# Half of the GRU's row transposes of layers one and two moved from TensorE to DMA, and the state update cut from three VectorE passes after z to two

## The chip, the cores and the metric

The kernel runs on one core of one Trainium2 chip. The metric is the device time of one execution in microseconds (us), as the median of several runs. Beside those runs one execution was profiled; every row of a profile and every duration below is from that one execution. A core has TensorE (PE in the profile, with its weight loads as PEld), VectorE (DVE), ScalarE (ACT), GpSimd (POOL) and SyncE (SP), which here only issues DMAs. They run their own instruction streams in order and wait for each other on semaphores.

## The reference, cut to what matters

There are 64 graphs of 256 nodes with 256 features. Four graph layers follow each other; each normalises `x`, applies relu, computes its layer and adds it to `x`. Layers 0, 1 and 2 are attention layers (4 heads, 4 heads, 1 head). Layer 3, in which the change lies, has three rounds of message passing with a GRU cell:

```python
def _gru_cell(inp, h, w_ih, w_hh, b_ih, b_hh):
    gi = inp @ w_ih.T + b_ih
    gh = h @ w_hh.T + b_hh
    i_r, i_z, i_n = jnp.split(gi, 3, axis=-1)
    h_r, h_z, h_n = jnp.split(gh, 3, axis=-1)
    r = jax.nn.sigmoid(i_r + h_r)
    z = jax.nn.sigmoid(i_z + h_z)
    n = jnp.tanh(i_n + r * h_n)
    return (1.0 - z) * n + z * h
...
A = (adj != 0).astype(x.dtype)
h = x
for i in range(3):
    m = jnp.einsum('bnd,de->bne', h, weight[i])
    aggr = jnp.einsum('bst,bsd->btd', A, m)
    h = _gru_cell(aggr, h, w_ih, w_hh, b_ih, b_hh)
return h
...
h = jnp.maximum(_layernorm(x, axis=-1), 0.0)
x = x + _L3_gnn_ref(h, adj, ...)
```

## The kernel before, in words

The work is cut into 33 units: units 1 to 31 hold two graphs each (512 nodes, S = 512), units 0 and 32 hold one. `graphs(u, first, nb)` (line 1021) records all operations of a unit: `layer0`, `layer1`, `layer2`, then `gru`. Nothing is emitted while it records. Each operation has an engine, a written-down cost in ns and the buffers that it reads and writes; buffers come from classes with a fixed number of slots (lines 853 to 864: 8 PSUM banks, 8 slots `g` for the gate tiles, 2 slots `hl`, 1 slot `y`, 2 slots `tp`, 3 slots `pl`).

The order of the instructions on each engine is made by a planner, `_Schedule.run` (line 681). It gives each operation a due time, worked back from its unit's end (unit number times `PACE`), with `STRETCH` and `MARGIN` as allowances per step. Then it walks through a planned time: whenever an engine is free, it takes from the ready operations the one with the earliest due time whose buffers have a free slot (`roomy`, line 654). `HOP` is the assumed delay from the end of an operation to the start of one that waits for it. `GUARDED` names a buffer class in which a later unit must leave a slot free while an earlier unit still has to take one; `YIELD` belongs to VectorE operations that give way to others. The resulting order is fixed in the program; on the chip each engine runs its list in order. Several units are in progress at once (there are five slots for `xt`), so that TensorE always has matmuls of one unit while ScalarE and VectorE work on others.

**The GRU** (line 1442). The state is held transposed, features on partitions, in two halves of 128 features (j = 0 and 1), as `ht3_`. For each of three rounds (i = 0, 1, 2; the code's L, called layers of the GRU here) and each half, `unit` (line 1548) issues six `gate` operations (line 1483), each two 128x512 matmuls in fp32 (the profile shows two records for each): r and z each from the state (`whh`) and from the aggregate (`wc`), the candidate's two parts apart. ScalarE evaluates the tanh of each (line 874, `vec`), VectorE combines them. Sigmoid is written through tanh: with t = tanh(half of the argument), z = (1 + t)/2. The new state is stored as twice its value, 2h' = (1 + t) h + (1 - t) n.

For the next round the aggregate needs the state with nodes on partitions again. `rows_of` (line 1514) turns a half: on TensorE it issues four 128x128 transposes into a PSUM bank (line 1523). `split` (line 1448) then makes a high and a low part from it (`hl`: one ScalarE copy, line 1452, one VectorE subtraction), and `aggregate` (line 1458) multiplies both parts by the adjacency matrix in eight matmuls (line 1465).

The other way to turn a half exists already, `rows_turned` (line 1493). ScalarE copies the 128x512 fp32 words into two planes of 16 bits (`pl`, line 1502), SP issues a DMA transpose of both planes (`tp`, line 1503), ScalarE copies the planes back into words (`y`, line 1507). It is used in units 1 to 31 (`BACK`), for the last round's result, where `y` is added to `x` directly. The tuple `EARLY` names the halves for which it is used in the first two rounds as well; before the change it is empty. The layers before the GRU turn their normalised rows in the same way (lines 1113, 1115, 1119).

**The normalisation** (`norm`, line 1035) of layers 0, 1 and 2 subtracts the mean of each 128-row chunk and applies relu: chunks named in `CENTRED` on VectorE (line 1053), the others on ScalarE (line 1057). The normalisation in front of the GRU scales on ScalarE always (line 1063).

```python
                    vec(stt, dve(683), lambda: by_chunk(d.tile), lambda: by_chunk(z.tile), 1.0,
                        lambda: block(ht, j), op0=OP.add, op1=OP.mult,
...
                    vec(stt, dve(683), lambda: n.tile, lambda: z.tile, -1.0, lambda: n.tile,
                        op0=OP.add, op1=OP.mult, reads=[z], writes=[n], port=True)
                    vec(stt, dve(683), lambda: h_new.tile[:, j, :], lambda: d.tile, 2 * half, lambda: n.tile,
                        op0=OP.mult, op1=OP.subtract, reads=[d, n], writes=[(h_new, j)], port=True)
```

These are the three VectorE passes after z (`d` = (t + 1) h, `n` = (t - 1) n, then the difference); the first and the second wait for z's tanh, the third for both.

Of the kernel before, what the change touches and what calls it, by code (L numbers as in the profile page):

```python
# [14 lines left out]
OP = mybir.AluOpType  # L15
# [505 lines left out]
TURNED = 3  # L521
ENDED = 1
CLOSED = 0
CENTRED = (0,1)
BACK = range(1, 32)
EARLY = ()
LIFTED = (0,2)
PACE = 101000.0


def _runs(numbers):
# [15 lines left out]
class _Op:  # L547
    __slots__ = (
        "engine", "cost", "port", "emit", "group", "bufs", "takes", "nbytes", "succs", "waits", "due", "ready",
        "index", "yields", "base", "grabs",  # L550
    )


class _Schedule:
# [9 lines left out]


    OVERLAP = {"pe": 0, "act": 97, "dve": 81, "pool": 0, "sp": 0}
    HOP = {"pe": 250, "act": 100, "dve": 200, "pool": 100, "sp": 0}
    DMA_LATENCY = 3500
    DMA_RATE = 220.0
    DMA_AHEAD = 2000  # L570
    RESERVE = {"dve": 1.0, "act": 1.03}
    STRETCH = 2.0
    MARGIN = 1600
    YIELD = 20000.0
    GUARDED = ("wh",)

    def __init__(self, tc, pools):

# [8 lines left out]
        return _Buf(cls, shape, dtype, tile)  # L587

    def op(self, engine, cost, emit, reads=(), writes=(), takes=(), nbytes=0, port=False, yields=False,
           grabs=False):  # L590
        o = _Op()
        o.port, o.yields, o.grabs = port or grabs, yields, grabs
        o.engine, o.base, o.emit, o.group, o.nbytes = engine, cost, emit, self.group, nbytes
        o.cost = cost * self.RESERVE.get(engine, 1.0)
        o.succs, o.index, o.ready = [], len(self.ops), 0.0
        deps, o.bufs, o.takes = set(), [], []
        for written, items in ((False, reads), (True, writes)):
            for item in items:
                b, part = item if isinstance(item, tuple) else (item, None)
                if b not in o.bufs:  # L600
                    o.bufs.append(b)
                    b.left += 1
                if written and b.tile is None and b not in o.takes:
                    o.takes.append(b)
                keys = list(b.parts) if part is None else [k for k in (part, None) if k in b.parts]
                for k in keys:
                    writer, readers = b.parts[k]
                    if writer is not None:
                        deps.add(writer)
                    if written:  # L610
                        deps.update(readers)
                writer, readers = b.parts.get(part, (None, []))
                if written:
                    if part is None:
                        b.parts.clear()
                    b.parts[part] = (o.index, [])
                else:
                    b.parts[part] = (writer, readers + [o.index])
        for b in takes:
            if b.tile is None and b not in o.takes:  # L620
                o.takes.append(b)
        deps.discard(o.index)
        o.waits = len(deps)
        for d in deps:
            self.ops[d].succs.append(o)
        self.ops.append(o)
        return o
# [26 lines left out]
    def roomy(self, o):  # L654
        need = {}
        for b in o.takes:
            if b.tile is None:
                need[b.cls] = need.get(b.cls, 0) + 1
        for c, n in need.items():
            if c in self.GUARDED and self.first_taker(c) < o.group:  # L660
                n += 1
            if len(self.free[c]) < n:
                return False
        return True
# [113 lines left out]
def _fast_path(  # L778
# [48 lines left out]
    slots = ctx.enter_context(tc.tile_pool(name="slots", bufs=1))  # L827
# [29 lines left out]
            "cap_n": (slots, 1), "xn": (slots, 4), "ht": (slots, 2), "wh": (slots, 3),  # L857
            "cb2_": (slots, 2), "cb1_": (slots, 1), "pt": (slots, 5), "o": (slots, 2),
            "ag": (slots, 2), "ht3_": (slots, 3), 
            "hl": (slots, 2), "am_r": (slots, 1), "g": (slots, 8), "y": (slots, 1), "f": (slots, 6),  # L860
            "st": (slots, 4), "mv": (slots, 5), "row": (slots, 3), "rs": (slots, 10),
            "mean": (slots, 4), "pl": (slots, 3), "tp": (slots, 2), "rd": (dram, 4), "bank": (banks, 8),
        },
    )
# [5 lines left out]
    def bank(dtype=F32):  # L870
        return buf("bank", [P, S * 4 // mybir.dt.size(dtype)], dtype)

    def vec(fn, cost, *args, reads=(), writes=(), engine="dve", port=False, yields=False, grabs=False, **kw):
        emit = lambda: fn(*[a() if callable(a) else a for a in args], **kw)  # L874
        op(engine, cost, emit, reads, writes, port=port, yields=yields, grabs=grabs)


    sched.group = -1
# [142 lines left out]
    def graphs(u, first, nb):  # L1021
# [420 lines left out]
        def gru(pair):  # L1442
# [33 lines left out]
            def by_chunk(ap):  # L1476
                return ap.rearrange("p (c n) -> p c n", n=P)
# [5 lines left out]
            def gate(ps, w, B_w, g, v, first, last):  # L1483
                def emit():
                    for dc in range(DC):
                        nc.tensor.matmul(  # L1486
                            by_chunk(ps.tile[:, :S]), lhsT=w[:, dc, g * P : (g + 1) * P], rhs=block(v, dc),
                            start=(first and dc == 0), stop=(last and dc == DC - 1),
                        )

                op("pe", pe(1717), emit, [v, B_w], [ps])

            def rows_turned(ht, j, last):

# [39 lines left out]
            def g_tile():  # L1534
                return buf("g", [P, S])
# [6 lines left out]
            for i in range(L):  # L1542
                last = i == L - 1
                h_new = buf("ht3_", [P, DC, S])
                wi = wc[:, i]
                stt = nc.vector.scalar_tensor_tensor

                def unit(j, ht, ag, h_new, wi, half):
                    r, n, d, z = (g_tile() for _ in range(4))
                    ps_r, ps_h, ps_i, ps_z = (bank() for _ in range(4))  # L1550
                    gate(ps_r, whh, B_whh, j, ht, True, False)
                    gate(ps_h, whh, B_whh, 4 + j, ht, True, True)
                    vec(nc.scalar.activation, act(682), lambda: n.tile, lambda: ps_h.tile[:, :S], AF.Identity,
                        bias=bg[:, 4 + j : 5 + j], scale=half, reads=[ps_h, B_bg], writes=[n], engine="act")
                    gate(ps_r, wi, B_wc, j, ag, False, True)
                    vec(nc.scalar.activation, act(682), lambda: r.tile, lambda: ps_r.tile[:, :S], AF.Tanh,
                        bias=bg[:, j : j + 1], scale=half, reads=[ps_r, B_bg], writes=[r], engine="act")
                    vec(stt, dve(683), lambda: n.tile, lambda: r.tile, 1.0, lambda: n.tile,
                        op0=OP.add, op1=OP.mult, reads=[r], writes=[n], port=True)
                    gate(ps_i, wi, B_wc, 4 + j, ag, True, True)  # L1560
                    vec(stt, dve(685), lambda: n.tile, lambda: ps_i.tile[:, :S], 2 * half, lambda: n.tile,
                        op0=OP.mult, op1=OP.add, reads=[ps_i], writes=[n])
                    vec(nc.scalar.activation, act(712), lambda: n.tile, lambda: n.tile, AF.Tanh,
                        bias=bg[:, 6 + j : 7 + j], reads=[B_bg], writes=[n], engine="act")
                    gate(ps_z, whh, B_whh, 2 + j, ht, True, False)
                    gate(ps_z, wi, B_wc, 2 + j, ag, False, True)
                    vec(nc.scalar.activation, act(682), lambda: z.tile, lambda: ps_z.tile[:, :S], AF.Tanh,
                        bias=bg[:, 2 + j : 3 + j], scale=half, reads=[ps_z, B_bg], writes=[z], engine="act")
                    vec(stt, dve(683), lambda: by_chunk(d.tile), lambda: by_chunk(z.tile), 1.0,
                        lambda: block(ht, j), op0=OP.add, op1=OP.mult,  # L1570
                        reads=[z, ht if len(ht.shape) == 4 else (ht, j)], writes=[d], port=True)
                    vec(stt, dve(683), lambda: n.tile, lambda: z.tile, -1.0, lambda: n.tile,
                        op0=OP.add, op1=OP.mult, reads=[z], writes=[n], port=True)
                    vec(stt, dve(683), lambda: h_new.tile[:, j, :], lambda: d.tile, 2 * half, lambda: n.tile,
                        op0=OP.mult, op1=OP.subtract, reads=[d, n], writes=[(h_new, j)], port=True)

                for j in range(DC):
                    unit(j, ht, ag, h_new, wi, 0.5 if i == 0 else 0.25)
                ag = None if last else buf("ag", [P, DC, S])
                for j in range(DC):  # L1580
                    hl = rows_of(h_new, j, last)
                    if not last:
                        aggregate(ag, [hl], j, lambda k, b, sc, hl=hl: hl.tile[:, k, 2 * b + sc, :])
                ht = h_new
# [85 lines left out]
```

## Time and profile before

| | us |
|---|---|
| median of 3 runs | 3029.45 (3028.26 to 3031.09) |
| the profiled execution, whole | 3031.28 |
| its span, first to last instruction | 3029.5 |
| granted TensorE clock, mean over the span | 0.997 |

| steady stretch, 500 to 2500 us | busy us of 2000 |
|---|---|
| PE | 2000.00 |
| DVE | 1554.03 |
| ACT | 1560.36 |
| POOL | 182.78 |

How to read the rows of the profile: a group is a line of the kernel, an engine, an operation and its tiles (`out<-in`, buffer numbers left out), then how often it occurs, its busy time, the mean duration of one in ns, and the engine's idle time just before it with what ended it. Most ScalarE and VectorE operations are issued through the helper `vec` and so stand under line 874; they are told apart by their tiles. PE records overlap, since a matmul's record lasts longer than the distance to the next one.

### The profile page before, as it was taken

What the parts mean: (1) busy time and instruction counts of PE and PEld (TensorE: products, weight loads), DVE (VectorE), ACT (ScalarE), POOL (GpSimd) and SP (SyncE); (2) the same over time, 40 slices, a digit from 0 to 9 for tenths busy, and PEclk for the clock granted to TensorE, in tenths of its full rate; (3) what the DMA queues carried; (4) which work ended last, traced back from release to release, by engine and by line L of the source; (5) the groups of instructions that cost most, each with busy time, mean ns of one, the idle gap of its engine ahead of it and who ended that gap; (6) DMA issues with size and microseconds to landing.
All of it is one profiled execution on the core that took longest, in us unless ns stands there. A gap on an engine that the chain in (4) does not pass through costs nothing.

```text
span 3029.5 us, 47896 instructions
## 1 busy us (share of the span) xinstructions
PE 2996.4 (99%) x17423; PEld 1813.7 (60%) x17423; DVE 2307.4 (76%) x5702; ACT 2260.7 (75%) x4123; POOL 283.2 (9%) x317
## 2 busy tenths in 40 slices
PE   7999999999999999999999999999999999999998
PEld 6865556656565656565656566555556565656556
DVE  8977887777877777887778877778877778877653
ACT  6867777787878788787787877877787877766544
POOL 2101010001100011000010100010010010100000
PEclk9999999999999999999999999999999999999999
DMA  4222222323323322232232223233233222221110
GB/s 140 76 64 65 60 74 74 90 69 78 72 64 84 85 67 74 70 81 77 68 94 60 74 74 91 69 82 72 59 84 84 68 72 68 65 67 46 39 30 19
DMA packets 429321, 215.86 MB, mean 71 GB/s; under 512 B 356170, under 2 KB 408980, under 8 KB 429076
## 3 DMA queue, kind: packets, MB, share of 16 engines
q1 hardware_dynamic: 425104, 211.36, 28.1%
q8 instruction: 139, 2.28, 0.3%
q10 hardware_dynamic: 3972, 1.36, 0.2%
q14 instruction: 106, 0.87, 0.1%
HBM read 109.84 MB, written 17.34 MB: 42 GB/s over the span
## 4 chain that ended last, share of the span: by engine, by line
PE 98%; DVE 1%; ACT 1%; DMA 0%; issue 0%; SPq 0%; ACTq 0%; DVEq 0%
PE bank L1486 65%; PE bank L1269 12%; PE bank L1137 11%; PE bank L1465 6%; PE bank L1523 2%; PE bank L994 1%; PE bank L1192 0%; PE bank L1172 0%; PE bank L1098 0%; DMA at<-in_adj_dram 0%; DVE o L874 0%; DVE pt L874 0%; DVE pt L1234 0%; ACT pt L1243 0%; DVE g L874 0%
## 5 line engine op out<-in xcount | busy, mean ns | idle before, releaser
L1486 PE MATMUL bank<-ht,whh 128*128 128x512 f32 (+1 forms) x2376 | 1052.8, 580 | 0.0
L1486 PE MATMUL bank<-ag,wc 128*128 128x512 f32 (+1 forms) x2376 | 1050.4, 580 | 0.0
L1486 PEld LDWEIGHTS bank<-ag,wc 128*128 128x128 f32 x2376 | 448.7, 190 | 524.4 <-issue 509.1
L1486 PEld LDWEIGHTS bank<-ht,whh 128*128 128x128 f32 x2376 | 441.5, 191 | 481.5 <-issue 451.7
L874 ACT ACTIVATE g<-bank,bg 128x512 f32<-128x512 f32 (+1 forms) x594 | 392.6, 671 | 207.3 <-PE bank L1486 202.7
L874 DVE SCALAR_TENSOR_TENSOR g<-g,g 128x512 f32<-128x512 f32 (+1 forms) x396 | 265.7, 671 | 264.5 <-ACT g L874 262.8
L1269 PE MATMUL bank<-wh,pt 128*64 128x65 f32 (+1 forms) x8704 | 372.3, 232 | 0.1
L1269 PEld LDWEIGHTS bank<-wh,pt 128*64 128x64 f32 (+1 forms) x8704 | 340.8, 141 | 50.3 <-POOL mean L874 20.5
L1243 ACT ACTIVATE pt<-cb,f 128x256 f32<-128x256 f32 x620 | 322.8, 590 | 0.6 <-DMA cb<-rd 0.6
L1119 ACT COPY ht<-tp 128x1024 uint16<-128x1024 uint16 x232 | 306.8, 1339 | 0.9 <-DMA tp<-pl 0.5
L874 DVE SCALAR_TENSOR_TENSOR pt<-pt,f,cap 128x256 f32<-128x256 f32 x620 | 264.7, 481 | 2.8 <-ACT pt L1243 2.6
L1147 ACT ACTIVATE wh<-bank,mv 128x264 f32<-128x264 f32 (+1 forms) x384 | 177.2, 479 | 85.8 <-PE bank L1137 85.1
L1465 PE MATMUL bank<-am_r,hl 128*128 128x256 f32 x1536 | 234.7, 302 | 0.9 <-ACT hl L1452 0.6
L1113 ACT COPY pl<-xn 128x1024 uint16<-128x1024 uint16 x232 | 234.9, 1036 | 0.8
L874 POOL TENSOR_TENSOR mv<-mv,nhalf 128x4 f32<-128x4 f32 (+1 forms) x132 | 136.9, 1044 | 1022.9 <-DVE mv L874 765.1
L1042 DVE BATCH_NORM_STATS2 st<-xt 128x6 f32<-128x256 f32 x512 | 207.1, 404 | 20.6 <-DMA xt<-in_x_dram 20.4
L1465 PEld LDWEIGHTS bank<-am_r,hl 128*128 128x128 f32 x1536 | 197.9, 189 | 28.0 <-issue 22.0
L874 DVE SCALAR_TENSOR_TENSOR g<-bank,g 128x512 f32<-128x512 f32 (+1 forms) x198 | 133.4, 674 | 102.0 <-PE bank L1486 100.8
L874 ACT ACTIVATE g<-g,bg 128x512 f32<-128x512 f32 (+1 forms) x198 | 139.5, 705 | 95.7 <-DVE g L874 94.8
L1234 DVE TENSOR_SCALAR pt<-cb,f 128x256 f32<-128x256 f32 x532 | 184.2, 408 | 31.9 <-DMA cb<-rd 30.0
L874 DVE SCALAR_TENSOR_TENSOR g<-g,ht 128x512 f32<-128x512 f32 (+1 forms) x198 | 133.2, 673 | 91.4 <-ACT g L874 91.2
L874 ACT COPY ag<-bank 128x512 f32<-128x512 f32 (+1 forms) x198 | 110.1, 572 | 84.0 <-PE bank L1465 83.0
(96 smaller groups left out, 3222.4 us busy)
## 6 DMA issues: line engine op xcount, KB each, us to landing
cb<-rd SPq DMA_DIRECT2D x120, 512.0 KB
xt<-in_x_dram SPq DMA_DIRECT2D x31, 512.0 KB
at<-in_adj_dram SPq DMA_DIRECT2D x31, 512.0 KB
out_dram<-xt SPq DMA_DIRECT2D x31, 512.0 KB
cb<-rd SPq DMA_DIRECT2D x34, 256.0 KB
tp<-pl SPq DMA_TRANSPOSE x294
cap<-cap_n SPq DMA_TRANSPOSE x128
rd<-row ACTq DMA_DIRECT2D x60, 8.0 KB
```

The lines of the kernel that those rows point to most:

```text
L874: emit = lambda: fn(*[a() if callable(a) else a for a in args], **kw)
L1042: nc.vector.bn_stats(st.tile[:, c, :], xt.tile[:, c, :])
L1113: op("act", 1040, lambda: nc.scalar.copy(pl.tile, planes(xns[b].tile.rearrange("p c d -> p (c d)"))), [xns[b]], [pl])
L1119: op("act", 1330, lambda: nc.scalar.copy(planes(ht.tile[:, 2 * b : 2 * b + 2].rearrange("p c d n -> p (c d n)")), tp.tile,), [tp], [(ht, b)])
L1137: nc.tensor.matmul(ps.tile[:, : heads * W], lhsT=ht.tile[:, c, dc, :], rhs=we[:, dc].rearrange("p h w -> p (h w)"), start=(dc == 0), stop= ...
L1147: op("act", 470, lambda: nc.scalar.activation(wh.tile[:, :, c, :], ps.tile[:, : heads * W].rearrange("p (h w) -> p h w", h=heads), AF.Iden ...
L1234: nc.vector.tensor_scalar(pt.tile[:, b, jc, :].rearrange("p (i n) -> p i n", n=P), cb.tile[:, k, 2 * b : 2 * b + 2, :], f.tile[:, 1, h, c ...
L1243: op("act", 590, lambda: nc.scalar.activation(view().rearrange("p (i n) -> p i n", n=P), cb.tile[:, k, 2 * b : 2 * b + 2, :], AF.Relu, sca ...
L1269: nc.tensor.matmul(ps[q * Q : (q + 1) * Q], lhsT=pt.tile[:, b, jc, i0 : i0 + Q], rhs=wh.tile[:, h, 2 * b + jc, :w], start=(jc == 0), stop= ...
L1465: nc.tensor.matmul(ps.tile[:, b * N : (b + 1) * N], lhsT=rows(k, b, sc), rhs=am.tile[:, 2 * b + sc, :], start=(k == 0 and sc == 0), stop=( ...
L1486: nc.tensor.matmul(by_chunk(ps.tile[:, :S]), lhsT=w[:, dc, g * P : (g + 1) * P], rhs=block(v, dc), start=(first and dc == 0), stop=(last a ...
L1523: nc.tensor.transpose(ps.tile[:, c * P : (c + 1) * P], ht.tile[:, j, c * P : (c + 1) * P], ident)
```

## The change

What it does:

- `EARLY = (0,)`: in units 1 to 31, half j = 0 is turned by `rows_turned` in the first two rounds too. Half j = 1 stays on TensorE.
- `unit` writes the state as 2h' = (t + 1)(h - n) + 2n. The difference `d` is made before z's tanh and lies in r's tile; after z two passes are left. The number of VectorE passes in a unit stays five. `unit` takes three `g` tiles in place of four; `leave` makes n's first operation wait in the plan until three `g` slots are free, and r's until two are.
- `CENTRED = ()`: the chunks 0 and 1 of the three attention layers' normalisations go from VectorE to ScalarE.
- The planner: `PACE` 101000 to 98000, `HOP` of PE 250 to 300, `STRETCH` 2 to 1, `YIELD` 20000 to 5000; `wh` is guarded no more; in the new class `STRICT`, which holds `hl`, no operation of a later unit takes a slot while an earlier unit still has to take one. `y` gets a second slot, `mv` a sixth. `LEAVE` is 0.

```diff
-CENTRED = (0,1)
+CENTRED = ()
 BACK = range(1, 32)
-EARLY = ()
+EARLY = (0,)
 LIFTED = (0,2)
-PACE = 101000.0
+LEAVE = 0
+PACE = 98000.0
...
-    HOP = {"pe": 250, "act": 100, "dve": 200, "pool": 100, "sp": 0}
+    HOP = {"pe": 300, "act": 100, "dve": 200, "pool": 100, "sp": 0}
...
-    STRETCH = 2.0
+    STRETCH = 1.0
     MARGIN = 1600
-    YIELD = 20000.0
-    GUARDED = ("wh",)
+    YIELD = 5000.0
+    GUARDED = ()
+    STRICT = ("hl",)
...
         for c, n in need.items():
-            if c in self.GUARDED and self.first_taker(c) < o.group:
+            n += o.leave
+            if (c in self.GUARDED or c in self.STRICT) and self.first_taker(c) < o.group:
+                if c in self.STRICT:
+                    return False
                 n += 1
             if len(self.free[c]) < n:
                 return False
...
-            "hl": (slots, 2), "am_r": (slots, 1), "g": (slots, 8), "y": (slots, 1), "f": (slots, 6),
-            "st": (slots, 4), "mv": (slots, 5), "row": (slots, 3), "rs": (slots, 10),
+            "hl": (slots, 2), "am_r": (slots, 1), "g": (slots, 8), "y": (slots, 2), "f": (slots, 6),
+            "st": (slots, 4), "mv": (slots, 6), "row": (slots, 3), "rs": (slots, 10),
...
-                    r, n, d, z = (g_tile() for _ in range(4))
+                    r, n, z = (g_tile() for _ in range(3))
+                    d = r
...
+                    vec(stt, dve(683), lambda: by_chunk(d.tile), lambda: block(ht, j), 2 * half,
+                        lambda: by_chunk(n.tile), op0=OP.mult, op1=OP.subtract,
+                        reads=[n, ht if len(ht.shape) == 4 else (ht, j)], writes=[d], port=True)
                     gate(ps_z, whh, B_whh, 2 + j, ht, True, False)
                     gate(ps_z, wi, B_wc, 2 + j, ag, False, True)
                     vec(nc.scalar.activation, act(682), lambda: z.tile, lambda: ps_z.tile[:, :S], AF.Tanh,
                         bias=bg[:, 2 + j : 3 + j], scale=half, reads=[ps_z, B_bg], writes=[z], engine="act")
-                    vec(stt, dve(683), lambda: by_chunk(d.tile), lambda: by_chunk(z.tile), 1.0,
-                        lambda: block(ht, j), op0=OP.add, op1=OP.mult,
-                        reads=[z, ht if len(ht.shape) == 4 else (ht, j)], writes=[d], port=True)
-                    vec(stt, dve(683), lambda: n.tile, lambda: z.tile, -1.0, lambda: n.tile,
-                        op0=OP.add, op1=OP.mult, reads=[z], writes=[n], port=True)
-                    vec(stt, dve(683), lambda: h_new.tile[:, j, :], lambda: d.tile, 2 * half, lambda: n.tile,
-                        op0=OP.mult, op1=OP.subtract, reads=[d, n], writes=[(h_new, j)], port=True)
+                    vec(stt, dve(683), lambda: d.tile, lambda: z.tile, 1.0, lambda: d.tile,
+                        op0=OP.add, op1=OP.mult, reads=[z], writes=[d], port=True)
+                    vec(stt, dve(683), lambda: h_new.tile[:, j, :], lambda: n.tile, 2.0, lambda: d.tile,
+                        op0=OP.mult, op1=OP.add, reads=[n, d], writes=[(h_new, j)], port=True)
```

More of the change, by code (lines that the diff above doesn't have):

```diff
@@ L549 @@
         "engine", "cost", "port", "emit", "group", "bufs", "takes", "nbytes", "succs", "waits", "due", "ready",
-        "index", "yields", "base", "grabs",
+        "index", "yields", "base", "grabs", "leave",
     )
@@ L589, in op @@
     def op(self, engine, cost, emit, reads=(), writes=(), takes=(), nbytes=0, port=False, yields=False,
-           grabs=False):
+           grabs=False, leave=0):
         o = _Op()
+        o.leave = leave
         o.port, o.yields, o.grabs = port or grabs, yields, grabs
@@ L871, in bank, with vec @@
         return buf("bank", [P, S * 4 // mybir.dt.size(dtype)], dtype)
-    def vec(fn, cost, *args, reads=(), writes=(), engine="dve", port=False, yields=False, grabs=False, **kw):
+    def vec(fn, cost, *args, reads=(), writes=(), engine="dve", port=False, yields=False, grabs=False, leave=0, **kw):
         emit = lambda: fn(*[a() if callable(a) else a for a in args], **kw)
-        op(engine, cost, emit, reads, writes, port=port, yields=yields, grabs=grabs)
+        op(engine, cost, emit, reads, writes, port=port, yields=yields, grabs=grabs, leave=leave)
     sched.group = -1
@@ L1489, in emit @@
                         )
-                op("pe", pe(1717), emit, [v, B_w], [ps])
+                op("pe", pe(1717), emit, [v, B_w], [ps], leave=0 if last else LEAVE)
             def rows_turned(ht, j, last):
@@ L1553, in unit @@
                     vec(nc.scalar.activation, act(682), lambda: n.tile, lambda: ps_h.tile[:, :S], AF.Identity,
-                        bias=bg[:, 4 + j : 5 + j], scale=half, reads=[ps_h, B_bg], writes=[n], engine="act")
+                        bias=bg[:, 4 + j : 5 + j], scale=half, reads=[ps_h, B_bg], writes=[n], engine="act", leave=2)
                     gate(ps_r, wi, B_wc, j, ag, False, True)
                     vec(nc.scalar.activation, act(682), lambda: r.tile, lambda: ps_r.tile[:, :S], AF.Tanh,
-                        bias=bg[:, j : j + 1], scale=half, reads=[ps_r, B_bg], writes=[r], engine="act")
+                        bias=bg[:, j : j + 1], scale=half, reads=[ps_r, B_bg], writes=[r], engine="act", leave=1)
                     vec(stt, dve(683), lambda: n.tile, lambda: r.tile, 1.0, lambda: n.tile,
```

## The prediction

> **What bounds the kernel now.** I read the page first: busy shares and the chain that ended last.
>
> ```profile
> PE 2996.4 (99%) x17423; PEld 1813.7 (60%) x17423; DVE 2307.4 (76%) x5702; ACT 2260.7 (75%) x4123; POOL 283.2 (9%) x317
> ...
> PE 98%; DVE 1%; ACT 1%; DMA 0%; issue 0%; SPq 0%; ACTq 0%; DVEq 0%
> PE bank L1486 65%; PE bank L1269 12%; PE bank L1137 11%; PE bank L1465 6%; PE bank L1523 2%; PE bank L994 1%; PE bank L1192 0%; PE bank L1172 0%; PE bank L1098 0%; DMA at<-in_adj_dram 0%; DVE o L874 0%; DVE pt L874 0%; DVE pt L1234 0%; ACT pt L1243 0%; DVE g L874 0%
> ```
>
> 98% of the chain is TensorE; L1523, the transposes in question, hold 2%. A busy PE can hide waits, so I checked stretches and the longest pieces of the chain in order of time.
>
> ```profile
> 0.00:110.00 110.00, 89.37 (x859) 75.22 (x860) 95.02 (x298) 79.72 (x214) 25.61 (x39) 0.94 0.44 126
> ...
> 500.00:2500.00 2000.00, 2000.00 (x11623) 1187.10 (x11623) 1554.03 (x3797) 1560.36 (x2785) 182.78 (x197) 1.00 0.31 75
> ...
> 2850.00:3029.50 179.50, 167.19 (x709) 101.09 (x707) 87.85 (x206) 77.26 (x137) 5.61 (x9) 0.99 0.09 22
> ```
>
> ```profile
> 1360.83 20.60 PE bank L1486 x48
> ...
> 1452.68 20.60 PE bank L1486 x48
> ...
> 1544.52 20.60 PE bank L1486 x48
> ```
>
> The columns of the stretches after the length are busy us of PE, PEld, DVE, ACT and POOL, then clock and DMA share. From 500 to 2500 us PE is never idle, and the same piece returns every 91.85 us: one unit. The 512-column records start 429 ns apart there with almost no spread, so no wait hides in them. All of PE's 33 us idle lie at the ends: 20.6 in the first 110 us, 12.3 in the last 180. So only two things move the time: PE work, and new waits of PE.
>
> **What is removed from PE.** 31 units x 2 rounds x 1 half = 62 blocks of four transposes. The order of the changed program agrees: 9834 matmuls become 9586, 248 fewer. Price, from the timeline of PE:
>
> ```profile
> 2931.51 0.60 PE L1523 MATMUL bank<-ident,ht 128*128 128x128 f32 x4
> 2931.94 1.04 PE L1137 MATMUL bank<-w2e,ht 128*128 128x258 f32 x4
> ```
>
> The record lasts 0.60 us, but the next work starts 0.43 us after it. Start to start over all 520 transposes the median is 109 ns, so 62 x 4 x 0.109 = 27.0 us, or 0.87 us of each unit's 91.85. [...] By the page the sum would be 68 us, by start-to-start 27.0. I take 27.0.
>
> **What is added to ScalarE, VectorE and SP.** The same steps stand in the trace for the last round (views of the lines, shapes apart):
>
> ```profile
> L1507 ACT COPY y<-tp 128x1024 uint16<-128x1024 uint16 x62 | 82.9, 1338 | 0.0
> L1502 ACT COPY pl<-ht 128x1024 uint16<-128x1024 uint16 x62 | 64.7, 1044 | 80.5 <-DVE ht L874 80.5
> L1057 ACT ACTIVATE xn<-xt,mv 128x256 f32<-128x256 f32 x186 | 87.9, 497 | 4.6 <-DVE mv L874 3.9 <-DMA rd<-row 0.6
> L874 DVE TENSOR_SCALAR xn<-xt,mv 128x256 f32<-128x256 f32 x198 | 61.2, 340 | 3.2 <-ACT pl L1113 3.0
> L874 DVE SCALAR_TENSOR_TENSOR ht<-g,g 128x512 f32<-128x512 f32 x186 | 125.5, 687 | 2.2
> ```
>
> ACT gains 62 x (1.338 + 1.044) = 148 us for the planes and 198 x 0.497 = 98 us for the centring; DVE loses 198 x 0.340 = 67 us and gets six small negations of about 0.2 us in the one-graph units. Per unit: ACT 71.65 + 2 x 2.38 + 6 x 0.497 = 79.4 us of a period of 90.98, that is 78% before and 87% after; DVE about 69.5 us, 76%. Neither becomes the bound by its sum. SP issues 62 more transposes of 1.23 us (row L1503), 76 us on a queue that now issues 422 of them, about 520 us of 3029. A waiting transpose on SP holds the loads and the broadcasts `cb` behind it; VectorE's `pt` waits 30 us in all for `cb` now, none of it passed on to PE. The move adds 62 x 0.26 = 16 MB to 211 MB on that queue: its share goes from 28% to about 30%.
>
> [...] By the trace too the block is dearer in engine time: 0.43 us of PE against 2.38 us of ACT and 1.23 us of SP. If that lay on the path, the 148 us of ACT would make 3150 us. But PE is the engine with no idle time and ACT has 20 us of it per unit, so I count PE's loss alone.
>
> **Whether PE will wait for the turned half.** Chain from the last z gate to the aggregate: tanh 0.68, two passes 1.38, `pl` 1.04, DMA, `y` 1.34, `hl` 0.59 and 0.68. From the issue to the start of the copy behind it, the trace's 294 transposes into `tp` show 3.8 us at least, 6.9 in the median, 9.2 in nineteen of twenty, 13.1 at most. Sum 9.5 to 18.8 us, 12.6 in the median, some 0.5 more for hand-overs. I counted how much PE work the changed order puts between the last z gate and the aggregate of the turned half, with start-to-start distances of the trace: 18.1 to 20.6 us in the 52 blocks of the middle. That covers the median by 5 us and the nineteenth of twenty by 2.7. For the half that stays on PE it is 9.5 us or more (5.3 before) against 0.68 + 1.38 + 0.44 + 1.27 = 3.8. So in the middle I take 1 us of new waits in all; bounds 0 and, if ACT's queue is often late, more than the gain (below).
>
> **The two passes.** DVE's work stays five passes of 0.69 us; one moves ahead of z's tanh. After z the chain is 0.69 us shorter, which PE doesn't see in the middle, as it doesn't wait there. It sees it in the last unit, where nothing covers it: PE waits 1.79, 1.79 and 1.45 us at the ends of the rounds, and a half-size pass is 0.42 us, so about 1.3 us are won. The order also gives PE in units 30 and 31 new exposed places: half j = 1 is wanted 0.44 us and 1.7 us after its last gate where 2.3 are needed (1.9 + 0.6 us), and unit 31's turned halves have 11.2 and 12.5 us of cover against 13.1 (0 to 5 us, I take 2). Net for the end +3 us. For the start the same kinds of wait remain (first input 7.6 us, issue 4.2): 0, with 4 us either way. `STRICT`, `leave`, `PACE` and the rest change only the order, and are in these counts.
>
> **Sum.** Against the profiled execution's 3031.28 us: -27.0 + 1 + 3 + 0 = -23, so 3008.3; its span 3029.5 becomes 3006.5. The runs' median lies 1.8 us below the profiled time, at the span: 3029.45 - 23 = 3006.
>
> **Rivals.**
> - *As summed* (chance 0.76): 2999 to 3014 us, from the bounds of the ends and of waits up to 0.3 us per unit.
> - *The gain is eaten, no measurable change* (0.09): ACT at 87% of an in-order queue hands back PSUM banks late now and then. At 0.65 to 1.05 us of PE wait per unit (20 to 33 us) the time is 3026 to 3036, say 3029. For it: ACT's idle time per unit shrinks from 20 to 11.6 us. Against it: the order's distances grew, and before, PE waited for none of 31 units.
> - *Slower* (0.13): the turned half is late. A place: the first aggregate of rounds two and three, PE standing behind `hl`, whose ScalarE copy stands in the same queue behind `y`, which waits for the DMA, and behind both the next gates' tanh that free the banks. If SP issues late, because an earlier transpose or `cb` waits ahead of it, the chain reaches the 18.8 us that the slowest transposes give, and a queue delay of two ACT operations (1.3 us each) on top makes 21.4 against 18.1 to 20.6: some 1 us per block, 62 us, less 27 and with the ends +39: 3068. It decides from 0.44 us per block (27/62). Against it: the median has 5 us to spare.
> - *The change does not do what it says* (0.02): the order shows the transposes gone; only the profile's clock could then differ, 3029.
>
> Range: 2998 to 3027, which takes in the ends' bounds and half of the middle case. 0.2% (6 us) is about what a measurement of this kernel can tell from no change: faster 0.77, within 0.10, slower 0.13.
>
> **What would show it.** Right: L1523 with 272 records; unit period about 90.98 us; PE idle near 36 us and at the ends; ACT near 2500 us busy, DVE near 2245; `y` x124. Wrong: PE idle in the middle before L1465 with `hl` as releaser (the slower rival), before L1486 with ACT `g`, `wh` or `ag` (banks handed back late), or an end of over 20 us idle.

## The result and the profile after

| | before | after |
|---|---|---|
| median of 6 runs each, us | 3028.9 (3027.1 to 3031.1) | 3010.9 (3009.8 to 3011.7) |
| ratio with its 95% interval | | 0.9941 (0.9928 to 0.9953) |
| profiled execution, whole / span, us | 3031.28 / 3029.5 | 3010.84 / 3009.0 |
| PE busy / idle over the span, us | 2996.4 / 33.1 | 2972.5 / 36.5 |
| ACT busy, DVE busy, us | 2260.7, 2307.4 | 2435.3, 2286.4 |
| changes of kind on PE, 500 to 2500 us | 526 | 613 |

A kind is a line of the kernel with its tiles and shape, all gate matmuls (`whh` and `wc`) taken as one; a change of kind is a place where the next matmul on PE is of another kind.

The changed kernel is faster by 18 us. The measured 3010.9 us lies inside the predicted range, 5 us behind the predicted time. In the two profiled executions the span fell by 20.5 us: PE's busy time fell by 23.9, and its idle time rose by 3.4. The profiled execution of the kernel before was 2.4 us longer than the median of its runs, that of the kernel after lies at its median; so 2.5 of the 5 us belong to the execution that the prediction started from, and 2.5 to its terms.

The page of the kernel after: first the busy shares, then the engines of the chain that ended last.

```profile
PE 2972.5 (99%) x17175; PEld 1780.5 (59%) x17175; DVE 2286.4 (76%) x5510; ACT 2435.3 (81%) x4445; POOL 295.5 (10%) x317
...
PE 97%; DVE 2%; ACT 1%; DMA 0%; issue 0%; SPq 0%; ACTq 0%; DVEq 0%
```

There are exactly 248 matmul records fewer than before (17423 to 17175), and PE is still the bound. The same stretches as before the change (length, then busy us of PE, PEld, DVE, ACT and POOL, then clock and DMA share):

```profile
0.00:110.00 110.00, 86.47 (x855) 72.28 (x856) 91.06 (x285) 84.89 (x226) 24.44 (x39) 0.95 0.43 121
...
500.00:2500.00 2000.00, 2000.00 (x11484) 1172.88 (x11483) 1553.32 (x3684) 1688.94 (x3032) 199.59 (x198) 1.00 0.36 82
...
2850.00:3009.00 159.00, 147.00 (x579) 89.13 (x577) 77.25 (x181) 77.93 (x131) 6.03 (x8) 0.99 0.12 28
```

In the middle PE has no idle time after the change either, while ACT went from 1560 to 1689 of 2000 us, 78% to 84.4%. All the same, a unit did not become shorter by the whole 0.87 us. The longest pieces of the chain (start, length) show it:

```profile
1163.46 24.03 PE bank L1492 x56
...
1345.65 24.03 PE bank L1492 x56
```

This piece returns once in two units now: 182.19 us, 91.10 per unit, where before it was 91.85 and the prediction said 90.98. The missing 0.12 us per unit are inside PE's busy time. The added steps, by the view of the lines with shapes apart:

```profile
L1513 ACT COPY y<-tp 128x1024 uint16<-128x1024 uint16 x124 | 163.9, 1334 | 0.0
L1508 ACT COPY pl<-ht 128x1024 uint16<-128x1024 uint16 x124 | 128.5, 1036 | 36.3 <-DVE ht L880 35.8
L1529 PE MATMUL bank<-ident,ht 128*128 128x128 f32 x272 | 42.7, 277 | 5.6 <-DVE ht L880 5.0 <-DVE rs L880 0.6
```

The counts are those of the prediction, 124 copies of each kind and 272 transposes left; the mean durations agree to about 1%.

### The profile page after: what moved, and what is told of

Read it like the earlier page. It is cut to its first block, busy times and chain, and to the rows that moved or that the text cites. A ratio compares the mean times of both kernels' runs of the same rounds, so it can differ in the third digit from the quotient of the medians.

```text
span 3009.0 us, 47645 instructions
## 1 busy us (share of the span) xinstructions
PE 2972.5 (99%) x17175; PEld 1780.5 (59%) x17175; DVE 2286.4 (76%) x5510; ACT 2435.3 (81%) x4445; POOL 295.5 (10%) x317
## 3 DMA queue, kind: packets, MB, share of 16 engines
q1 hardware_dynamic: 490576, 227.62, 32.9%
## 4 chain that ended last, share of the span: by engine, by line
PE 97%; DVE 2%; ACT 1%; DMA 0%; issue 0%; SPq 0%; ACTq 0%; DVEq 0%
PE bank L1492 66%; PE bank L1275 12%; PE bank L1143 11%; PE bank L1471 6%; PE bank L1529 1%; PE bank L1000 0%; PE bank L1198 0%; DVE o L880 0%; PE bank L1104 0%; DVE g L880 0%; DVE pt L880 0%; PE bank L1178 0%; DMA w0e<-in_L_gnn_W_dram 0%; DVE pt L1240 0%; ACT pt L1249 0%; DVE ht L880 0%
## 5 line engine op out<-in xcount | busy, mean ns | idle before, releaser
L1492 PE MATMUL bank<-ag,wc 128*128 128x512 f32 (+1 forms) x2376 | 1061.6, 581 | 0.0
L880 DVE SCALAR_TENSOR_TENSOR pt<-pt,f,cap 128x256 f32<-128x256 f32 x620 | 275.0, 485 | 35.2 <-ACT pt L1249 34.5
L1471 PE MATMUL bank<-am_r,hl 128*128 128x256 f32 x1536 | 241.6, 307 | 0.7 <-ACT hl L1458 0.5
L1471 PEld LDWEIGHTS bank<-am_r,hl 128*128 128x128 f32 x1536 | 198.8, 190 | 47.4 <-issue 37.3
L880 POOL TENSOR_TENSOR mean<-mean,nhalf 128x8 f32<-128x8 f32 (+1 forms) x66 | 134.9, 2063 | 788.2 <-DVE mean L880 755.5
L880 DVE SCALAR_TENSOR_TENSOR g<-ht,g 128x512 f32<-128x512 f32 (+1 forms) x198 | 132.4, 670 | 85.3 <-ACT g L880 85.1
```

The source lines that it names most:

```text
L1471: nc.tensor.matmul(ps.tile[:, b * N : (b + 1) * N], lhsT=rows(k, b, sc), rhs=am.tile[:, 2 * b + sc, :], start=(k == 0 and sc == 0), stop=( ...
L1492: nc.tensor.matmul(by_chunk(ps.tile[:, :S]), lhsT=w[:, dc, g * P : (g + 1) * P], rhs=block(v, dc), start=(first and dc == 0), stop=(last a ...
```

## The experiments

Two theories stood against each other. Theory one: the time is PE's own work, so a removed transpose counts with its start-to-start distance, and what ScalarE, SP and the DMA do in its place is free while PE does not wait. Theory two: what decides is the order on the in-order queues and the cover that it leaves. The medians below stand beside runs of the kernel before on the same chip (3027.4 to 3028.0 us); ratios are to it. "ACT, middle" is ScalarE's busy share from 500 to 2500 us, and "unit" is the distance from one unit to the next there.

| run | us | ratio (95%) | ACT, middle | unit, us |
|---|---|---|---|---|
| before_less_four | 3006.7 | 0.9929 (0.9916 to 0.9943) | 78.6% | 90.99 and 91.30 |
| after_bare | 3010.6 | 0.9940 (0.9927 to 0.9954) | 79.9% | 91.10 |
| planes_twice | 3062.6 | 1.0115 (1.0099 to 1.0130) | 87.6% | 92.77 |
| both_halves | 3191.9 | 1.0539 (1.0525 to 1.0553) | 83.1% | 98.3 |
| early_alone | 3365.2 | 1.1113 (1.1096 to 1.1130) | 73.8% | 103.4 |
| two_pass_alone | 3042.9 | 1.0049 (1.0034 to 1.0064) | 76.8% | 92.33 |
| order_alone | 3364.1 | 1.1108 (1.1091 to 1.1125) | 71.6% | 103.1 |
| centred_dve | 3016.0 | 0.9961 (0.9948 to 0.9975) | 82.3% | 91.31 |
| no_early | 3152.9 | 1.0416 (1.0400 to 1.0432) | 76.6% | 95.9 |
| old_constants | 3286.6 | 1.0857 (1.0841 to 1.0874) | 75.5% | 100.1 |
| three_pass | 3025.0 | 0.9989 (0.9980 to 0.9997) | 84.3% | 91.3 |
| one_chunk_hop350 | 3011.2 | 0.9944 (0.9931 to 0.9958) | 83.1% | 91.22 |

The first three keep the order of the kernel that they start from and change only what is done at one place. The nine others let the planner make a new order.

**before_less_four**: the kernel before, in its order, with no transposes for half 0 of the first two rounds.

```diff
-                    for c in range(C):
+                    for c in range(0 if bare else C):   # bare = u in BACK and not last and j == 0
...
+                if bare:
+                    return split(lambda: by_chunk(ht.tile[:, j, :]), True, [ps])
```

> The kernel before in its own order, with the four TensorE transposes of half 0 left out in rounds one and two of units 1 to 31 (248 in all); the high and low parts are made from the untransposed half, so that part of the computation is left out. Nothing is added on any engine. If TensorE's work alone sets the time and a transpose is worth its start-to-start distance of 109 ns: -27 us, 3002, unit period 90.91 to 90.98 us. If a transpose were worth its record's 274 ns: -68 us, 2961. If TensorE's busy rows hide waits on others: less than -15 us.

Its chain's longest pieces:

```profile
1168.31 20.60 PE bank L1486 x48
...
1259.30 20.60 PE bank L1486 x48
...
1350.60 20.60 PE bank L1486 x48
```

The distances alternate: 90.99 and 91.30 us. In every second unit the eight transposes left out gave back 91.85 - 90.99 = 0.86 us, the 8 x 0.109 of the prediction. At 274 ns the unit would have lost 2.2 us. In the unit between, PE meets a new wait of 0.3 us before a transpose of the `row` chain (L1192, for ScalarE's `wh`): the removed 0.44 us of PE work had covered it. So PE work that goes away takes cover from short chains beside it, and of 27 us some 22 arrived in the span (3029.5 to 3007.9) even with nothing put in its place.

**after_bare**: the kernel after, in its order, with the two copies and the DMA transpose of the first two rounds not issued.

```diff
-                op("act", 1040, lambda: nc.scalar.copy(pl.tile, planes(ht.tile[:, j, :])), [(ht, j)], [pl])
+                op("act", 1040, lambda: bare or nc.scalar.copy(...), [(ht, j)], [pl])   # bare = not last; tp and y alike
```

> The changed kernel in its own order, with the added ScalarE copies and DMA transposes of half 0 left out in rounds one and two (the high and low parts come from the untransposed half, so that part of the computation is left out). ScalarE has 148 us less to do, SP 62 transposes less. Theory one, the added work lies under TensorE's and the missing part of the gain is due to the order: 3009 to 3011, as the changed kernel's 3010.9. Rival, ScalarE's load eats part of the gain: 3001 to 3005.

ScalarE's busy time fell by 130 us to 2305, and PE's stayed at 2972.6: 3010.6 against 3010.9 us, the unit 91.10 in both. In this order the added work costs nothing, which is theory one. The 0.12 us per unit that are missing are there without that work, so they belong to the order.

**planes_twice**: the kernel after, in its order, with the two added copies issued twice.

```diff
-                op("act", 1040, lambda: nc.scalar.copy(pl.tile, ...), [(ht, j)], [pl])
+                op("act", 1040, lambda: [nc.scalar.copy(pl.tile, ...) for _ in range(1 if last else 2)], [(ht, j)], [pl])
...
-                op("act", 1330, lambda: nc.scalar.copy(planes(...), tp.tile), [tp], [y])
+                op("act", 1330, lambda: [nc.scalar.copy(planes(...), tp.tile) for _ in range(1 if last else 2)], [tp], [y])
```

> The changed kernel in its own order, with the two ScalarE copies of each early-turned half made twice: ScalarE gains another 148 us (about 90% of a steady unit), the chain to the aggregate another 2.4 us. Theory one, TensorE's cover of 18 us holds: +0 to +6 us, 3011 to 3017. Rival, ScalarE is already the second bound: +15 us or more, with TensorE idle ahead of the aggregates.

It cost 52 us against the changed kernel. The stretch of the middle, and lines from PE's waits over the whole span (us in all, times, longest):

```profile
500.00:2500.00 2000.00, 1980.82 (x11254) 1148.51 (x11253) 1536.30 (x3632) 1751.41 (x3058) 174.72 (x193) 1.00 0.35 80
```

```profile
...
PE bank L1275 <- ACT wh L1153: 7.3, 13, 0.9
PE bank L1530 <- ACT row L1205: 5.8, 12, 0.7
...
PE bank L1492 <- ACT wh L1153: 4.8, 14, 0.4
```

No wait for `hl`, the end of the longer chain, is among the large ones. PE waits for `wh` and `row`: short ScalarE steps of other units that stand behind the doubled copies and that feed PE or hand a bank back. In the profiled executions the span grew by 50.1 us: 26.9 as idle time of PE and 23.2 inside its busy time, with the same matmuls in the same order. Short waits can hide there, since one record reaches over the next (a gate's record lasts some 592 ns in the profile before, the next starts after 429). ScalarE still had 12% of its time free. Whether the load or the longer blocks in its queue decide was not told apart; either way the margin that was free at 84.4% was gone at 87.6%, and counting the cover of the turned chain alone, as theory one did, missed it.

**both_halves**: `EARLY = (0, 1)` in the kernel after.

```diff
-EARLY = (0,)
+EARLY = (0, 1)
```

> The changed kernel with both halves turned by DMA in the first two rounds (EARLY = (0, 1)); the planner makes a new order. TensorE loses another 248 transposes, 27 us; ScalarE gains 148 us, to some 90% of a unit. The order leaves 13.3 us of TensorE work at least behind the last gate, against a chain of 12.6 in the median. Theory one: most of the second 27 us comes, 2988 to 3000. Rival, ScalarE or the DMA is late: no gain over the changed kernel, 3011 or more.

Another 248 transposes gone, and 181 us lost. PE is busy 1882 of 2000 us in the middle. It waits at the aggregate (L1471) for DVE's `o` (43.5 us in 6 waits, the longest 8.3) and for `wh` (28.7 in 7), both steps of attention layers, and at the gates for `ag` (22.0 in 11). The longest of these waits (start, length, engine, line, what):

```profile
913.15 1.29 DVE L880 TENSOR_TENSOR hl<-y,hl 128x512 fp32r<-128x512 f32 x2
...
920.60 1.39 DVE L880 TENSOR_TENSOR o<-bank,rs 128x256 f32<-128x256 f32 x4
...
921.14 1.19 PE L1471 MATMUL bank<-am_r,hl 128*128 128x256 f32 x4 [8.29 <-DVE o L880]
```

The aggregate's own input `hl` was ready at 914.4, 6.7 us before the wait ended. The steps named, `o<-bank` and `wh<-bank`, read a PSUM bank, so the likely reading is a bank that came back late; no run tested it. The time fits the rival (no gain), but at these waits the turned half was not what came last. What delays the attention layer's steps in the new order was not traced.

**early_alone**: the kernel before with `EARLY = (0,)`, with the second slot of `y`, the sixth of `mv` and `STRICT`. So this is not the moved transposes quite alone.

```diff
-EARLY = ()
+EARLY = (0,)
+    STRICT = ("hl",)
-            "hl": (slots, 2), ... "y": (slots, 1), ... "mv": (slots, 5), ...
+            "hl": (slots, 2), ... "y": (slots, 2), ... "mv": (slots, 6), ...
...
```

> The kernel before with half 0 turned by DMA in the first two rounds, and of the planner only what an order then needs: STRICT for hl, two slots y, six mv. Three passes after z, centring of two chunks on VectorE, PACE, HOP, STRETCH, YIELD as before. TensorE loses the same 248 transposes. Theory one (the removed work decides): about 3007, as with the transposes merely left out. Theory two (the order decides whether the gain is kept): chains counted against TensorE's work in this order leave 66 places between 500 and 2500 us with too little cover, some 2 to 3 us in each unit: 3050 to 3090, slower than before.

The direction is that of theory two, the size is far larger: +338 us. Two thirds of it are one wait, 9 us once per unit, 225 us in 26 waits, before the transposes of the half that stays on PE. PE's busy time also rose, by 53 us, though 27 us of work are gone; the last section has the granted clock beside it. The timeline of one wait:

```profile
1470.69 1.05 ACT L1508 COPY pl<-ht 128x1024 uint16<-128x1024 uint16 x1 [0.38 <-ACT row L1205]
1471.64 2.08 ACT L1069 ACTIVATE xn<-xt,mv 128x256 f32<-128x256 f32 x4
...
1472.52 0.68 DVE L880 SCALAR_TENSOR_TENSOR g<-bank,g 128x512 f32<-128x512 f32 x1
...
1473.62 0.62 ACT L880 ACTIVATE g<-o 128x512 f32<-128x512 f32 x1
1474.14 1.98 ACT L1119 COPY pl<-xn 128x1024 uint16<-128x1024 uint16 x2
...
1476.02 0.72 ACT L880 ACTIVATE g<-g,bg 128x512 f32<-128x512 f32 x1
...
1477.11 0.66 DVE L880 SCALAR_TENSOR_TENSOR g<-g,g 128x512 f32<-128x512 f32 x1
...
1478.28 0.68 DVE L880 SCALAR_TENSOR_TENSOR ht<-g,g 128x512 f32<-128x512 f32 x1
...
1479.11 1.08 PE L1529 MATMUL bank<-ident,ht 128*128 128x128 f32 x4 [9.13 <-DVE mean L880]
```

PE ended its last matmul at 1469.98 (1479.11 less 9.13). The candidate's sum is ready on VectorE at 1473.2 (`g<-bank,g`), after steps of an attention layer in the same list. Its tanh starts on ScalarE only at 1476.02, 2.8 us later, since `xn` and `pl` of another unit stand ahead of it. VectorE's two last steps, 1477.11 and 1478.28, again have a step of layer one between them. The row names `mean` as what ended the wait, because it ended last just before; what the transposes read is `ht`, which ends 0.1 us earlier. No engine is overloaded (ScalarE 73.8% in the middle): by this timeline it is the places in the lists; no run moved a single step to show it.

**two_pass_alone**: the kernel before with the two passes, three `g` tiles and `leave`; `STRICT` and the extra slots are in too, and `wh` isn't guarded.

```diff
-    GUARDED = ("wh",)
+    GUARDED = ()
+    STRICT = ("hl",)
...
-                    r, n, d, z = (g_tile() for _ in range(4))
+                    r, n, z = (g_tile() for _ in range(3))
+                    d = r
...
```

> The kernel before with the state made in two passes after z alone (with leave, STRICT for hl and without the guard of wh, which its order needs); all halves turned on TensorE as before, planner constants as before. TensorE's work is unchanged, VectorE has five passes as before. No place in the middle of this order lacks more than 0.1 us of cover: 3022 to 3036, no measurable change; a gain of more than 6 us would mean that the shorter chain was worth something in the middle.

Slower by 15.5 us, a little beyond the expected range. PE is idle only 1.5 us in the middle; the unit is 0.48 us longer, nearly all of it inside PE's busy time. Call the usual start-to-start distance between two matmuls of one kind its plain distance. Over the 2000 us the distances exceed the plain ones by some 10 us more than in the kernel before, with 647 changes of kind in place of 526.

**order_alone**: the kernel before with the changed constants, guards (`STRICT` among them), slots and `CENTRED = ()`, but `EARLY` empty and three passes.

```diff
-CENTRED = (0,1)
+CENTRED = ()
-PACE = 101000.0
+PACE = 98000.0
-    HOP = {"pe": 250, ...}
+    HOP = {"pe": 300, ...}
-    STRETCH = 2.0
+    STRETCH = 1.0
-    YIELD = 20000.0
-    GUARDED = ("wh",)
+    YIELD = 5000.0
+    GUARDED = ()
+    STRICT = ("hl",)
...
```

> The kernel before with the planner's part of the change alone: PACE, HOP, STRETCH, YIELD, guards, slots and the centring on ScalarE. Transposes and passes as before. If the new constants by themselves make a better order: below 3022. If they only fit the changed work: 30 places in the middle lack cover, 11 us in all by the chains alone, more with queues: 3040 to 3120.

3364 us, beyond the expectation again. The waits are spread: `hl` 52.5 us in 13, `pt` 45.2 in 35, `o` 31.7 in 12.

**old_constants** is its mirror: the kernel after with the four old constants and the old `CENTRED`.

```diff
-CENTRED = ()
-PACE = 98000.0
+CENTRED = (0,1)
+PACE = 101000.0
-    HOP = {"pe": 300, ...}
-    STRETCH = 1.0
-    YIELD = 5000.0
+    HOP = {"pe": 250, ...}
+    STRETCH = 2.0
+    YIELD = 20000.0
```

> The changed kernel with the constants of before: PACE 101000, HOP 250, STRETCH 2, YIELD 20000, two chunks centred on VectorE. The early turning, the two passes, leave and STRICT stay. No place in the middle of this order is short of cover by its own chain of operations. If those chains decide: 3002 to 3014. If the place in the engines' queues decides (TensorE then stands at one step of each unit while the tanh that it needs stands behind other units' copies on ScalarE): above 3050.

3286.6 us; PE waits 168 us in 52 waits for DVE's `pt`, before the attention matmuls, up to 6.1 us each. The change edits nothing in that chain.

**no_early**: the kernel after with `EARLY = ()`.

```diff
-EARLY = (0,)
+EARLY = ()
```

> The changed kernel with EARLY empty again: two passes, centring on ScalarE and the new planner constants stay, all halves of the first two rounds are turned on TensorE. TensorE has 27 us more to do than the changed kernel. If the rest of the change is neutral: 3011 + 27 = 3038 at most, 3028 to 3038. If an order only fits the work it was made for, as in the run with the planner's part alone: above 3060. If the rest brings a gain by itself: below 3022.

3152.9 us: the largest of PE's waits is that of the transposes for `ht` (55.5 us in 45 waits). Had only the transposes come back, 3010.9 + 27 would have been 3038; 115 us are the order's.

**three_pass**: the kernel after with the three passes, four `g` tiles and no `leave`.

```diff
-                    r, n, z = (g_tile() for _ in range(3))
-                    d = r
+                    r, n, d, z = (g_tile() for _ in range(4))
...
```

> The changed kernel with three passes after z as before (and so no leave and four g tiles in a unit); early turning, centring on ScalarE and the new constants stay. The chain after z is 0.69 us longer, a g slot is held longer. If the two passes bring nothing in the middle: 3009 to 3020, the tail about 1 us longer. If they are what makes room for the turned half: above 3030.

3025.0 us, 14 slower than after and past the expected range. PE's busy time is 7.3 us higher and its idle time 6.2: of the latter 3.0 us lie after 2850 us, 1.8 between 2500 and 2850, and 1.4 in the first 110. So with three passes the rest of the change brings only 3 of the 18 us. Whether the shorter chain or the freer `g` slots do it can't be read from this run, as the order changes with both.

**centred_dve** and **one_chunk_hop350**: the kernel after with both chunks centred on VectorE again, and with one of them and a longer `HOP`.

```diff
-CENTRED = ()
+CENTRED = (0,1)
```

> The changed kernel with two of the chunks of the normalisation centred on VectorE again, as before; the planner makes a new order. ScalarE loses 6 x 0.5 us per unit, VectorE gains 6 x 0.34. TensorE's work is the same. If ScalarE's load costs nothing in the middle (theory one) the middle keeps its period of about 91 us and only the ends' order can differ: 3001 to 3012. If the centring on ScalarE was needed for the gain, because VectorE is the tighter engine: 3018 or more.

```diff
-CENTRED = ()
+CENTRED = (0,)
-    HOP = {"pe": 300, ...}
+    HOP = {"pe": 350, ...}
```

> The changed kernel with one chunk centred on VectorE, which takes ScalarE between the load of the changed kernel and that of the run with two chunks, and HOP of PE 350 in place of 300, which plans 50 ns more between a matmul and what waits for it. A try for a version that beats both: 3003 to 3009 if the wider hand-over removes the short waits of the middle; 3011 to 3018 if the finer mixing of matmul kinds costs as much again.

The first is 5 us slower than after, though ScalarE does 63 us less and PE never waits in the middle: PE's busy time is 5.4 us higher. Its 3016.0 us lie between the two expectations. The second equals after within its interval: it has 4 us less idle time at the start, 19.4 against 23.5, and a unit of 91.22 us. No complete version here beats the changed kernel.

## Why the prediction was right

The forecast was right in its mechanism for this order: PE's removed work set the gain, and the added work lay under PE's. Its sum for the span was 23 us and 20.5 came. By its terms:

- **-27.0 for the transposes.** Right. The price of 109 ns is what before_less_four gives in its undisturbed units (0.86 us for eight). At 274 ns, the mean record of L1523 in the profile before, it would have meant 68 us.
- **The added work is free.** Right in this order: after_bare. ScalarE gained 175 us, not 246, and VectorE lost 21, not 62. The sum took each record's whole length, but records that follow directly overlap: above, four `xn` of about 0.59 us (L1069, mean 590 ns in the profile after) fill 2.08 us. For VectorE the same overlap makes the moved `xn` worth 61 us, not 67, and other groups grew, `pt<-pt,f,cap` by 10 us. The DMA queue's share rose from 28.1% to 32.9%, a little more than the 30% of the prediction. ScalarE stood at 84.4%, not 87%; planes_twice shows that 87.6%, made of longer blocks, was no longer free.
- **+1 for waits in the middle.** Mis-sized: PE has none as idle time, but its busy time fell by 23.9 instead of 27.0, which is +3.1. It is the order's (after_bare has the same), and it goes with finer mixing: 87 more changes of kind in the 2000 us, and some 2.5 us more over the plain distances. One place can be read off the chain, where eight gate matmuls split an attention layer's 128 narrow ones once in two units:

```profile
1218.20 3.43 PE bank L1492 x8
...
1243.06 3.88 PE bank L1275 x128
...
1332.45 2.02 PE bank L1275 x64
1334.47 3.63 PE bank L1492 x8
1338.10 2.02 PE bank L1275 x64
```

  Split, the three pieces take 7.67 us; apart, the same work takes 3.43 + 3.88 = 7.31. That is 0.18 us per unit, where 0.12 are missing; other places must be shorter. The pieces have these lengths to 0.01 us in the other units looked at, so they aren't waits of changing length. A change of kind has no fixed price: 29 ns on average here, but 84 ns in two_pass_alone (10.2 us for 121 changes). No run altered the mixing alone, so the cause of the whole 3.1 us stays open.
- **0 for the start.** It became +2.9 us of idle time in the first 110 us. The first waits changed little in sum (9.4 and 2.7 us in place of 7.6 and 4.2). One wait near the end of this stretch makes most of it:

```profile
99.79 1.18 PE L1104 MATMUL bank<-ident,xn 128*128 128x128 f32 x4 [7.47 <-ACT xn L1069]
101.77 3.78 PE L1492 MATMUL bank<-ht,whh 128*128 128x256 f32 x8 [0.79 <-ACT ht L880]
```

  The one-graph unit 0 has to be normalised in front of its GRU, and PE has nothing else left; the steps for it stand among layer one of unit 1 on three engines. Before, four smaller waits stood there (0.99, 2.39, 0.59 and 0.32 us). The prediction's 0 rested on the same waits remaining; here one long wait took the place of four short ones, and +2.9 lies within its 4 us either way.
- **+3 for the end.** It became -0.3. The two exposed places of half 1 came as counted (1.9 and 0.6 predicted):

```profile
2911.62 0.63 PE L1529 MATMUL bank<-ident,ht 128*128 128x128 f32 x4 [1.80 <-DVE ht L880]
2938.93 0.63 PE L1529 MATMUL bank<-ident,ht 128*128 128x128 f32 x4 [0.59 <-DVE rs L880]
```

  The 2 us for unit 31's turned halves did not come: from issue to copy their transposes took 5.7 and 5.8 us (over all units 6.4 in the median and at most 16.1), and PE didn't wait for them. The last unit's waits are 3.7 us in place of 5.3, 1.6 less and not 1.3. Two waits of the kernel before that the sum left standing, 0.8 and 0.9 us, are gone too, and the stretch behind PE's last matmul is 0.7 us longer.

So -27.0 + 3.1 + 2.9 - 0.3 is -21.3, and 0.6 us of the rest stands in small waits between 110 and 500 us and 0.3 between 2500 and 2850: -20.5 with rounding. The misses of the three small terms are +2.1, +2.9 and -3.3; that they cancel in part is luck. What the forecast had right is the -27.0 and that nothing large stands against it.

**What the prediction had right only by looking at the finished order.** It said that `STRICT`, `leave`, `PACE` and the rest "change only the order, and are in these counts", and that the shorter chain after z is nothing that PE sees in the middle. For this one order the counts held. As statements on the parts they fell: against the kernel before, the moved transposes cost 338 us, the planner's part with the centring 337 and the two passes 15.5, all three with `STRICT` and the extra slots in; against the kernel after, the old constants with the old centring cost 276 us and the three passes 14. The parts don't add. No run has `STRICT` alone, so its own share isn't separated; two_pass_alone shows that it can stand in a kernel with the old constants at 15.5 us in all. The rival "slower" named the right kind of place, a chain that stands in ScalarE's queue behind copies, but for the wrong half: in early_alone it is the half that stays on PE. Why the planner's list comes out so different for each combination stays open.

## What to carry to other kernels

Where one engine is always busy, as PE was from 500 to 2500 us, price its work by start-to-start distances (109 ns for a transpose here, where the record lasts 274). Work moved to engines with idle time can be free; show it by leaving the added work out in the same order, as after_bare does (3010.6 us without it, 3010.9 with it). Where fixed lists are interleaved by a planner, an edit's parts have no price of their own: judge the finished order, place by place, by what stands ahead of each short step that the bound engine waits for, and search the planner's constants again after every edit. Load alone says little: ScalarE at 73.8% went with +338 us, at 84.4% with -18.

## What the runs showed of the hardware that was not expected

In early_alone a long wait of PE cost more than its own length. Stretches around the wait of 9.13 us shown above (the clock is the third number from the end):

```profile
1470.00:1472.00 2.00, 0.00 (x0) 0.00 (x0) 2.00 (x6) 1.62 (x5) 0.13 (x1) 1.00 0.02 4
1472.00:1479.00 7.00, 0.00 (x0) 0.00 (x0) 6.86 (x19) 6.97 (x11) 1.64 (x1) 0.50 0.90 218
1479.00:1482.00 3.00, 2.89 (x7) 1.89 (x8) 3.00 (x10) 1.90 (x5) 2.14 (x1) 0.50 0.54 105
...
1483.00:1487.00 4.00, 4.00 (x17) 2.33 (x16) 4.00 (x11) 4.00 (x7) 0.00 (x0) 1.00 0.00 0
```

In this wait the granted clock was 1.00 up to 1472, 2 us after PE's last matmul ended (1469.98), and 0.50 from there to 1482, about 3 us after PE had work again; from 1483 to 1487 it was 1.00. The four transposes at 0.50 took 1.08 us, against 0.60 in the profile before (at 2931.51) and 0.63 in that after (at 2911.62), both at 1.00. What sets the granted clock was not measured.

The mean granted clock over the span was 0.951 in early_alone, 0.964 in order_alone and 0.966 in old_constants, against 0.998 in the changed kernel. Against the kernel before, PE's busy time rose by 53 us in early_alone and by 123 in order_alone. The likely reading is that part of this is slower matmuls behind waits; how much was not separated, since short waits can hide in the busy time too. In planes_twice, whose waits for `wh` and `row` last at most 0.9 us, the clock of the middle is 1.00.
